# Layer 1 as full masked attention instead of a gather, and layer 3's aggregation as two float32r products instead of one float32 product

## The chip, the cores and the metric

The kernel runs on one core of one Trainium2 chip. The metric is the device time of one execution in microseconds (us). A time given for a kernel is the median of its runs.

## The reference, cut to what matters

There are N = 2708 nodes with D = 512 features, and an adjacency matrix `adj` of 2708x2708 floats in which most entries are zero. Four layers follow each other; each adds to `x` a function of `h = max(layernorm(x), 0)`. All is float32.

```python
# layer 0: inc = adj + head, head the 0/1 mask of adj divided by its row norm
x = x + (inc @ h) / sum(inc, -1)
# layer 1: 8 heads, key size 64; a = max(adj, eye)
atts = einsum('hqk,hmk->hqm', h @ Wq, h @ Wk) / 8
atts = softmax(atts - 1e16 * (1 - a), -1)            # 8 x 2708 x 2708
x = x + einsum('hqm,hmk,hko->qo', atts, h @ Wv, Wo)
# layer 2
g = relu(adj @ (h @ W1) + b1);  g = relu(adj @ (g @ W3) + b3)
x = x + tanh(g @ Wf + bf)
# layer 3: A is 1 where adj is not 0
x = x + (A @ (h @ W + b)) / sum(A, 0)[:, None]
```

In layer 1 the entries of `adj` are weights between 0.05 and 5.42, and the mask term multiplies their differences by 1e16. So in each row the softmax gives weight one to the node with the largest entry, as long as the two largest entries differ by more than the scores can.

## The kernel before, in words

The nodes are cut into 22 tiles of up to P = 128 (21 full ones and one of 20 rows), and into 6 blocks of up to BLK = 512 (five full ones and one of 148). The loops are written out by Python; a list scheduler orders each engine's instructions when the program is built. It prefers the instruction that stands earlier in the program among those whose inputs and buffers are there, and may take later ones while it waits. Each engine then runs its list in order. Pools (`tile_pool`) fix how many buffers a tile has (`bufs`); an instruction waits until a buffer is free. DMAs are issued by SP (`nc.sync`) and POOL (`nc.gpsimd`).

- **Preparation**: `value_weights` (L128) multiplies the value and output weights of layer 1 into one 512x512 matrix `wvo`; `square_sum` (L147) sums the squares of the query and key weights.
- **Layer 0**: first `h0` for all 22 tiles (to L535), then a loop over 22 node tiles `m`. VectorE makes `head` from the slab `at` (L555), counts (`part`, L557), TensorE adds the counts over partitions (`cnt`, L561), VectorE scales and adds (L564 to L574) and sums degrees (`dpart`, L576). TensorE then multiplies the slab with `h0`, 22 products into one accumulator (L583), and `x1` is written (L594).
- **Layer 1 in the same loop**: for tile `m`, the row slab `arow` of `adj` is loaded (L598), its largest entry and index are found (L601, L602), their lead is kept (L603, L611), and the new `x1` is normalised, transposed and multiplied with `wvo` (`accz`, L108), and written to `z` (L622). `alone` (L163) compares the smallest lead with what the scores could differ by, and sets `flag`. Then a loop gathers for each node the row of `z` that its largest entry names (L631), adds `x1` (L642) and writes `x2` (L643).
- **Layers 2 and 3** (`_layers_2_3`): `g1` (tiles of `norm_project`: layernorm, four transposes L102, four products L108); the first aggregation (`aggregate_relu`, L420), block by block, with the projection by `w3`; the second, with the projection by `wf`, tanh, `x3`, and `norm_project` by `w` into `g3`; then the third aggregation (L492) of `g3` with the 0/1 matrix `nz` (L489).
- At the end, `full_attention()` and a second `layers_2_3()` stand inside a conditional block that runs only where `flag` is 0. In the runs shown it isn't entered: no instruction of it is in the trace.

A float32 product is issued as two pairs of LDWEIGHTS and MATMUL; a transpose (a matmul against the identity) as one pair. So `x2112` records at L420 stand for 1056 products.

Of the kernel before, what the change touches and what calls it, by code (L numbers as in the profile page):

```python
# [8 lines left out]
FP = mybir.dt.float32  # L9
AF = mybir.ActivationFunctionType  # L10
# [9 lines left out]
TOP_SLACK = 2.0**-20  # L20
# [3 lines left out]
def kernel(  # L24
# [19 lines left out]

# [67 lines left out]
    z = dram.tile([N, D], FP, name="z")  # L117
    best = const.tile([P, NT, 8], mybir.dt.uint32, name="best")
    lead = const.tile([P, NT], FP, name="lead")
    nc.gpsimd.memset(lead, 1.0)  # L120
    flag = const.tile([1, 1], mybir.dt.int32, name="flag")

    def load_heads(pool, src, name):
        w = pool.tile([P, NCD, D], FP, name=name)
        for h in range(H):
            nc.sync.dma_start(
                out=w[:, :, h * DK : (h + 1) * DK],
                in_=src[h].rearrange("(c p) k -> p c k", p=P),  # L128
            )
        return w  # L130

    def value_weights(wvo, work, psum):

        wv = load_heads(work, wv_d, "wv")
        wo = load_w(work, wo_d, "wo")
        wvT = work.tile([P, NCD, D], FP, name="wvT")
        for c in range(NCD):
            pt = psum.tile([P, NCD, P], FP, name="ptr")
            for j in range(NCD):
                nc.tensor.transpose(pt[:, j, :], wv[:, j, c * P : (c + 1) * P], ident)  # L140
            nc.scalar.copy(wvT[:, c, :], pt.rearrange("p j k -> p (j k)"))
        for j in range(NCD):
            acc = psum.tile([P, D], FP, name="ptr")
            project(acc, wvT[:, :, j * P : (j + 1) * P], P, wo)
            nc.vector.tensor_copy(wvo[:, j, :], acc)

    def square_sum(work):  # L147

        squares = const.tile([P, 2], FP, name="squares")
        for i, (src, name) in enumerate(((wq_d, "wq"), (wk_d, "wk"))):  # L150
            w = load_heads(work, src, name)
            nc.scalar.activation(
                w.rearrange("p c k -> p (c k)"),
                w.rearrange("p c k -> p (c k)"),
                AF.Square,
                accum_out=squares[:, i : i + 1],
            )
        norm = const.tile([P, 1], FP, name="norm")
        nc.vector.tensor_add(norm, squares[:, 0:1], squares[:, 1:2])
        return norm  # L160

    def alone(norm, work, psum):

        total = psum.tile([P, 1], FP, name="ptr")
        nc.tensor.matmul(total, ones, norm, start=True, stop=True)
        least = work.tile([P, 1], FP, name="least")  # L170
        nc.vector.tensor_reduce(least, lead, AX.X, ALU.min)

        spare = work.tile([P, 1], FP, name="spare")
        nc.vector.scalar_tensor_tensor(
            spare,
            total,
            -1.01 * D * float(DK) ** -0.5 / MASK_SCALE,
            least,
            op0=ALU.mult,
            op1=ALU.add,  # L180
        )
        row = psum.tile([P, P], FP, name="ptr")
        nc.tensor.transpose(row[:1, :], spare, ident)
        worst = work.tile([1, 1], FP, name="worst")
        nc.vector.tensor_reduce(worst, row[:1, :], AX.X, ALU.min)
        nc.vector.tensor_scalar(flag, worst, 300.0 / MASK_SCALE, None, op0=ALU.is_gt)

    def full_attention():

        with tc.tile_pool(name="l1_qkv", bufs=1) as qkvp:  # L190
            qT = qkvp.tile([P, NCD, N], FP, name="qT")
            kT = qkvp.tile([P, NCD, N], FP, name="kT")
            v = qkvp.tile([P, NT, D], FP, name="v")
            wo = load_w(qkvp, wo_d, "wo")
            qk_scale = float(DK) ** -0.5

            with tc.tile_pool(name="l1_pw", bufs=1) as pwp, tc.tile_pool(
                name="l1_ph", bufs=2
            ) as php, tc.tile_pool(name="l1_px", bufs=3) as pxp, tc.tile_pool(
                name="l1_pps", bufs=2, space=PSUM  # L200
            ) as ps_tr, tc.tile_pool(name="l1_pacc", bufs=4, space=PSUM) as ps_acc:
                wq, wk, wv = (
                    pwp.tile([P, NCD, D], FP, name=name) for name in ("wq", "wk", "wv")
                )
                for w, src in ((wk, wk_d), (wq, wq_d), (wv, wv_d)):
                    for h in range(H):
                        nc.sync.dma_start(
                            out=w[:, :, h * DK : (h + 1) * DK],
                            in_=src[h].rearrange("(c p) k -> p c k", p=P),
                        )  # L210
                for b in range(NB):
                    c0 = b * BLK
                    nb = min(BLK, N - c0)
                    hT = php.tile([P, NCD, BLK], FP, name="hT")
                    tiles = range(c0 // P, (c0 + nb + P - 1) // P)
                    for t in tiles:
                        n = rows(t)
                        o = t * P - c0
                        xt = pxp.tile([P, D], FP, name="xt")
                        nc.sync.dma_start(out=xt[:n], in_=x1[t][:n])  # L220
                        hn = pxp.tile([P, D], FP, name="hn")
                        layernorm(pxp, xt, n, hn)
                        transpose_relu(ps_tr, hn, n, hT[:, :, o : o + n])
                    for dst, w, scale in ((kT, wk, None), (qT, wq, qk_scale)):
                        for oc in range(NCD):
                            acc = ps_acc.tile([P, BLK], FP, name="acc")
                            for c in range(NCD):
                                nc.tensor.matmul(
                                    acc[:, :nb],
                                    w[:, c, oc * P : (oc + 1) * P],  # L230
                                    hT[:, c, :nb],
                                    start=(c == 0),
                                    stop=(c == NCD - 1),
                                )
                            if scale is None:
                                nc.vector.tensor_copy(dst[:, oc, c0 : c0 + nb], acc[:, :nb])
                            else:
                                nc.scalar.mul(dst[:, oc, c0 : c0 + nb], acc[:, :nb], scale)
                    for t in tiles:
                        n = rows(t)  # L240
                        acc = ps_acc.tile([P, D], FP, name="acc")
                        project(acc, hT[:, :, t * P - c0 : t * P - c0 + n], n, wv)
                        nc.any.tensor_copy(v[:n, t, :], acc[:n])

            with tc.tile_pool(name="l1_bias", bufs=2) as bp, tc.tile_pool(
                name="l1_p", bufs=2
            ) as pp, tc.tile_pool(name="l1_pT", bufs=3) as ptp, tc.tile_pool(
                name="l1_x", bufs=1
            ) as xp, tc.tile_pool(name="l1_st", bufs=4) as stp, tc.tile_pool(
                name="l1_s", bufs=2, space=PSUM  # L250
            ) as ps_s, tc.tile_pool(name="l1_t", bufs=2, space=PSUM) as ps_t, tc.tile_pool(
                name="l1_o", bufs=1, space=PSUM
            ) as ps_o, tc.tile_pool(name="l1_y", bufs=1, space=PSUM) as ps_y:
                SW = 2 * BLK
                for m in range(NT):
                    n = rows(m)
                    cols = slice(m * P, m * P + n)

                    bias = bp.tile([P, N], FP, name="bias")
                    nc.sync.dma_start(out=bias[:n], in_=adj[cols])  # L260
                    xt = xp.tile([P, D], FP, name="xt", bufs=2)
                    nc.sync.dma_start(out=xt[:n], in_=x1[m][:n])
                    nc.vector.tensor_max(bias[:n, cols], bias[:n, cols], ident[:n, :n])
                    nc.vector.tensor_scalar(
                        bias[:n], bias[:n], 1.0, MASK_SCALE, op0=ALU.subtract, op1=ALU.mult
                    )
                    sums = stp.tile([P, H], FP, name="sums")
                    acc_o = ps_o.tile([P, D], FP, name="acc_o")
                    for h in range(H):
# [415 lines left out]
```

## Time and profile before

| | us |
|---|---|
| median of 3 runs | 2511.19 (2510.17 to 2511.49) |
| the profiled execution | 2511.49 |
| its span, first to last instruction | 2509.7 |
| busy in the span: PE / VectorE / ScalarE / POOL | 2185.8 / 896.2 / 172.5 / 76.3 |
| last `z` written by POOL (L622), start of the issue | 847.4 |
| first instruction of TensorE in layer 2 | 914.6 |
| last product of the first two aggregations' stage ends (L429) | 2049.7 |
| last product of layer 3 starts (L492) | 2491.8 |

The mean granted TensorE clock over the span is 0.918. A group of instructions is given by line, engine, operation and the names of what it writes and reads; the two figures behind it are its busy time in us and the mean length of one record in ns. TensorE's records overlap[...]; so the rate of a row of products is read from their starts, not from their lengths.

### The profile page before, as it was taken

The numbers are of one execution on the slowest core, as the hardware profiler recorded it, in microseconds if no ns is written. First come the engines' busy times: TensorE is split into PE (matmuls) and PEld (weight loads), VectorE is DVE, ScalarE is ACT, GpSimd is POOL, SyncE is SP. The second block draws the span as 40 slices with busy tenths as digits, with TensorE's granted clock in tenths as the row PEclk, the third lists the DMA queues.
The fourth block names the chain that finished last, engine by engine and source line by source line (L and its number), as shares of the span: only waits on it lengthen the run. The fifth ranks groups of instructions, "written<-read, shape, count | busy, mean of one in ns | idle before, by whom it ended". The sixth has DMA issues, their size and how long they took to land.

```text
span 2509.7 us, 13959 instructions
## 1 busy us (share of the span) xinstructions
PE 2185.8 (87%) x5331; PEld 968.8 (39%) x5331; DVE 896.2 (36%) x1243; ACT 172.5 (7%) x322; POOL 76.3 (3%) x142
## 2 busy tenths in 40 slices
PE   4776767877778449999999999999999999999997
PEld 2222323333333124444444464444444464444441
DVE  5999995556653153112111110210202021111111
ACT  2100000000000011000000000120202120000000
POOL 0000000000000210000000000000000000000000
PEclk8788878888888769999999999999999999999998
DMA  8545332112220471121222122221222121333311
GB/s 239 169 141 198 127 113 70 51 57 70 70 62 20 163 267 56 51 69 58 64 63 63 46 69 76 88 84 51 71 64 84 47 87 56 105 122 101 105 50 43
DMA packets 161867, 225.24 MB, mean 90 GB/s; under 512 B 23906, under 2 KB 88898, under 8 KB 159084
## 3 DMA queue, kind: packets, MB, share of 16 engines
q1 hardware_dynamic: 153232, 196.53, 25.5%
q0 software_dynamic: 8560, 27.74, 3.0%
q8 instruction: 44, 0.72, 0.1%
q14 instruction: 31, 0.25, 0.0%
HBM read 195.45 MB, written 28.78 MB: 89 GB/s over the span
## 4 chain that ended last, share of the span: by engine, by line
issue 61%; PE 27%; DVE 7%; DMA 3%; POOL 2%; SPq 0%; ACT 0%; POOLq 0%; DVEq 0%; ACTq 0%
PE agg L420 19%; PE pj L108 7%; DVE top L601 1%; DVE part L557 1%; DMA xt<-x 1%; DVE best L602 1%; PE ptr L108 1%; DVE stats L87 1%; DVE dpart L576 1%; DVE at L574 0%; POOL out_dram L505 0%; POOL x L469 0%; POOL x L594 0%; DVE hn L94 0%; PE ptr L102 0%
## 5 line engine op out<-in xcount | busy, mean ns | idle before, releaser
L420 PE MATMUL agg<-a,g 128*128 128x512 f32 (+3 forms) x2112 | 809.8, 543 | 0.0
L583 PE MATMUL acc<-h,at 128*128 128x512 f32 (+1 forms) x968 | 477.7, 645 | 202.1 <-DVE at L574 183.9
L420 PEld LDWEIGHTS agg<-a,g 128*128 128x128 f32 (+1 forms) x2112 | 376.6, 190 | 417.6 <-issue 417.6
L492 PE MATMUL agg<-g,nz 128*128 128x512 f32 x968 | 428.1, 600 | 0.0
L583 PEld LDWEIGHTS acc<-h,at 128*128 128x128 f32 (+1 forms) x968 | 186.5, 200 | 439.8 <-issue 233.8
L492 PEld LDWEIGHTS agg<-g,nz 128*128 128x128 f32 x968 | 176.3, 187 | 250.9 <-issue 244.3
L410 DVE TENSOR_SCALAR_CACHE_REDUCE nz<-a 128x512 f32<-128x512 f32 (+2 forms) x132 | 75.5, 618 | 336.4 <-DMA a<-in_adj_t_dram 336.2
L489 DVE TENSOR_SCALAR nz<-a 128x512 f32<-128x512 f32 (+2 forms) x132 | 52.0, 395 | 368.5 <-PE agg L492 347.3
L465 DVE TENSOR_TENSOR z<-pj,bf 128x512 f32<-128x512 f32 (+1 forms) x22 | 15.2, 691 | 409.2 <-PE pj L108 408.8
L108 PE MATMUL pj<-w,hTt 128*128 128x512 f32 (+1 forms) x352 | 157.4, 600 | 1.1 <-ACT hTt L103 1.0
L102 PE MATMUL ptr<-ident,hn 128*128 128x128 f32 (+1 forms) x264 | 44.3, 311 | 82.0 <-DVE hn L94 82.0
L557 DVE TENSOR_REDUCE part<-head 128x128 f32<-128x2816 f32 (+1 forms) x22 | 105.2, 4781 | 0.4
L576 DVE TENSOR_REDUCE dpart<-at 128x128 f32<-128x2816 f32 (+1 forms) x22 | 104.3, 4741 | 0.0
L108 PEld LDWEIGHTS pj<-w,hTt 128*128 128x128 f32 (+1 forms) x352 | 65.7, 188 | 87.4 <-issue 79.1
L429 ACT ACTIVATE hT<-agg,b 128x512 f32<-128x512 f32 (+1 forms) x48 | 29.8, 637 | 883.8 <-PE agg L420 803.2
L108 PE MATMUL accz<-wvo,hT 128*128 128x512 f32 (+1 forms) x176 | 88.3, 649 | 0.7 <-ACT hT L103 0.7
L108 PE MATMUL pj<-wf,hT 128*128 128x512 f32 (+1 forms) x176 | 88.3, 665 | 0.0
L102 PEld LDWEIGHTS ptr<-ident,hn 128*128 128x128 f32 (+1 forms) x264 | 36.9, 164 | 120.5 <-issue 120.1
L108 PE MATMUL pj<-w,hT 128*128 128x512 f32 (+1 forms) x176 | 82.3, 628 | 0.0
L589 DVE RECIPROCAL rdeg<-deg 128x1 f32<-128x1 f32 (+1 forms) x22 | 3.5, 159 | 209.6 <-PE deg L587 209.6
L574 DVE TENSOR_TENSOR at<-at,head 128x2816 f32<-128x2816 f32 (+1 forms) x22 | 65.5, 2976 | 0.0
L601 DVE MAX8 top<-arow 128x8 f32<-128x2708 f32 (+1 forms) x22 | 65.5, 2976 | 0.0
(77 smaller groups left out, 848.7 us busy)
## 6 DMA issues: line engine op xcount, KB each, us to landing
a<-in_adj_t_dram SPq DMA_DIRECT2D x105, 768.0 KB
arow<-in_adj_dram SPq DMA_DIRECT2D x21, 1354.0 KB
at<-in_adj_t_dram SPq DMA_DIRECT2D x21, 1344.0 KB
xt<-x SPq DMA_DIRECT2D x63, 256.0 KB
xt<-in_x_dram SPq DMA_DIRECT2D x42, 256.0 KB
x<-xo POOLq DMA_DIRECT2D x42, 256.0 KB, 3.8
z<-zo POOLq DMA_DIRECT2D x21, 256.0 KB, 2.3
x<-xo SPq DMA_DIRECT2D x21, 256.0 KB
```

Source lines behind the costliest of these rows:

```text
L102: nc.tensor.transpose(pt[:, c, :n], hn[:n, c * P : (c + 1) * P], ident[:n, :n])
L108: nc.tensor.matmul(acc[:n], hT[:, c, :n], w[:, c, :], start=(c == 0), stop=(c == NCD - 1))
L410: nc.vector.tensor_scalar(nz[:k, :nb], a[:k, :nb], 0.0, None, op0=ALU.not_equal, op1=ALU.add, accum_out=degp[:k, t, block : block + 1],)
L420: nc.tensor.matmul(accs[c][:, :nb], g[:k, t, c * P : (c + 1) * P], a[:k, :nb], start=(t == 0), stop=(t == NT - 1),)
L429: nc.scalar.activation(hT[:, c, :nb], accs[c][:, :nb], AF.Relu, bias=bias[:, c : c + 1])
L489: nc.vector.tensor_scalar(nz[:k, :nb], a[:k, :nb], 0.0, None, op0=ALU.not_equal)
L492: nc.tensor.matmul(accs[m][:n], nz[:k, o : o + n], g3[:k, t, :], start=(t == 0), stop=(t == NT - 1),)
L557: nc.vector.tensor_reduce(part[:, :n], head[:, :, :n].rearrange("p t m -> p m t"), AX.X, ALU.add)
L574: nc.vector.tensor_tensor(at[:, :, :n], at[:, :, :n], head[:, :, :n], ALU.add)
L576: nc.vector.tensor_reduce(dpart[:, :n], at[:, :, :n].rearrange("p t m -> p m t"), AX.X, ALU.add)
L583: nc.tensor.matmul(acc[:n], at[:k, t, :n], h0[:k, t, :], start=(t == 0), stop=(t == NT - 1))
L601: nc.vector.max(top[:n], arow[:n])
```

## The change

Three things change.

1. **Layer 0's loop is left with layer 0 alone.** The preparation, `arow` and its maximum, the layernorm, `accz`, `z`, `flag` and the gather are gone. The pools become deeper: `at` has 3 buffers instead of 2, `head` 2 instead of 1, `cnt` and `deg` 2 instead of 1.
2. **Layer 1 is computed in full, in the main line.** The body of `full_attention` stands where the gather stood, with no condition: for each block `q`, `k` (transposed) and `v` are projected; then for each tile `m` and each of 8 heads the scores of 128 nodes against 2708 are made in 3 pieces (K = 64 rows), VectorE adds the mask and takes the maximum, ScalarE the exponential, TensorE transposes the 22 pieces and multiplies each with its 64 columns of `v`. The conditional block is gone.
3. **Layers 2 and 3** have other pools, and layer 3 splits its features:

```diff
-        gp = es.enter_context(tc.tile_pool(name="g", bufs=2))
-        wp = es.enter_context(tc.tile_pool(name="wp", bufs=3))
-        hp = es.enter_context(tc.tile_pool(name="hp", bufs=2))
-        GRP = 3
+    gp = ctx.enter_context(tc.tile_pool(name="g", bufs=3))
+    wmats = ctx.enter_context(tc.tile_pool(name="wmats", bufs=2))
+    wp = ctx.enter_context(tc.tile_pool(name="wp", bufs=2))
+    hp = ctx.enter_context(tc.tile_pool(name="hp", bufs=1))
+    GRP = 2
...
-                norm_project(xo, rows(t), w, g3[: rows(t), t, :], bl)
+            acc = norm_project(xo, n, w)
+            hid = wp.tile([P, D], FP, name="hid")
+            nc.vector.tensor_add(hid[:n], acc[:n], bl[:n])
+            nc.scalar.copy(hi[:n, t, :], hid[:n])
+            nc.vector.tensor_sub(lo[:n, t, :], hid[:n], hi[:n, t, :])
...
-                nz = wp.tile([P, BLK], FP, name="nz", bufs=2)
+            nz = wp.tile([P, BLK], FR, name="nzr", tag="nz", bufs=2)
...
+            width = len(nodes) * P
+            if width > nb:
+                nc.gpsimd.memset(nz[:k, nb:width].bitcast(FP), 0.0)
             for m in nodes:
-                    n, o = rows(m), m * P - c0
-                    nc.tensor.matmul(
-                        accs[m][:n],
-                        nz[:k, o : o + n],
-                        g3[:k, t, :],
-                        start=(t == 0),
-                        stop=(t == NT - 1),
-                    )
+                o = m * P - c0
+                for half in (hi, lo):
+                    nc.tensor.matmul(
+                        accs[m],
+                        nz[:k, o : o + P],
+                        half[:k, t, :],
+                        start=(t == 0 and half is hi),
+                        stop=(t == NT - 1 and half is lo),
+                    )
         for m in nodes:
-                xo = wp.tile([P, D], FP, name="xo", bufs=4)
+            xo = wp.tile([P, D], FP, name="xf", tag="hid")
```

`hi` and `lo` are float32r (`FR`), both 22 tiles of 128x512. `hi` is the rounding of `hid` to float32r, `lo` what is left of it. The groups of adjacency tiles that one DMA brings shrink from 3 to 2. The loads of `wf` and `w` stand behind the first aggregation, since `wmats` has two buffers for four matrices.

The loop of one head, which now runs 22 x 8 = 176 times:

```python
for s0 in range(0, N, SW):                       # 1024, 1024 and 660 columns
    s = ps_s.tile([P, SW], FP, name="s")         # 2 buffers
    ...  # two products of up to 512 columns, K = 64
    nc.vector.tensor_add(p[:n, s0 : s0 + sw], s[:n, :sw], bias[:n, s0 : s0 + sw])
nc.vector.reduce_max(nmax[:n], p[:n], axis=AX.X)
nc.vector.tensor_scalar_mul(nmax[:n], nmax[:n], -1.0)
nc.scalar.activation(p[:n], p[:n], AF.Exp, bias=nmax[:n], accum_out=sums[:n, h : h + 1])
for t0 in range(0, NT, 4):                       # 6 groups of up to 4 pieces
    ...  # transposes into pt (2 buffers)
    copy = nc.scalar.copy if (t0 // 4) % 2 else nc.vector.tensor_copy
    ...  # copy pt to pT (3 buffers), then one product with v (64 columns) for each piece
```

`p` has 2 buffers, so that of three heads in a row the first must be transposed before the third's scores are stored.

## The prediction

> **What bounds the kernel now.** I read the page's slices first, then its groups, then the chain of waits for the rates of long rows of products, then the timeline of one step of layer 0 and of the gather.
>
> ```profile
> PE   4776767877778449999999999999999999999997
> DVE  5999995556653153112111110210202021111111
> PEclk8788878888888769999999999999999999999998
> ```
>
> Each digit is a 40th of 2509.7 us, 62.7 us. Up to slice 13 (840 us, layer 0) TensorE is neither full nor at full clock; slice 14 is the gather; from slice 15 on TensorE is full. So layers 2 and 3 are bound by TensorE; layer 0 isn't yet explained.
>
> ```profile
> L420 PE MATMUL agg<-a,g 128*128 128x512 f32 (+3 forms) x2112 | 809.8, 543 | 0.0
> L583 PE MATMUL acc<-h,at 128*128 128x512 f32 (+1 forms) x968 | 477.7, 645 | 202.1 <-DVE at L574 183.9
> L492 PE MATMUL agg<-g,nz 128*128 128x512 f32 x968 | 428.1, 600 | 0.0
> L557 DVE TENSOR_REDUCE part<-head 128x128 f32<-128x2816 f32 (+1 forms) x22 | 105.2, 4781 | 0.4
> L465 DVE TENSOR_TENSOR z<-pj,bf 128x512 f32<-128x512 f32 (+1 forms) x22 | 15.2, 691 | 409.2 <-PE pj L108 408.8
> L601 DVE MAX8 top<-arow 128x8 f32<-128x2708 f32 (+1 forms) x22 | 65.5, 2976 | 0.0
> ```
>
> The third figure is the idle time ahead of a group: L420 and L492 wait for nothing, layer 0's L583 waits 183.9 us for VectorE's `at`.
>
> ```profile
> 990.65 0.87 PE ptr L102 x8
> ...
> 1095.77 75.72 PE agg L420 x176
> ```
>
> The chain of waits gives rates: 176 records in 75.72 us, 0.430 us each, so 0.86 us for a float32 product of 512 columns (0.854 from record to record inside a row), and 0.109 us for a transpose.
>
> ```profile
> 532.19 0.38 PE L587 MATMUL deg<-ones,dpart 128*128 128x1 f32 x2
> 532.44 0.47 PE L561 MATMUL cnt<-part,ones 128*128 128x128 f32 x2
> 541.46 2.08 PE L583 MATMUL acc<-h,at 128*128 128x512 f32 x2 [8.56 <-DVE at L574]
> ...
> 566.63 0.47 PE L561 MATMUL cnt<-part,ones 128*128 128x128 f32 x2
> ```
>
> This timeline of TensorE is one step of layer 0: 34.2 us from `cnt` to `cnt`, with 8.56 us in which TensorE waits for VectorE's scaling (L564 to L574). VectorE had the next `part` ready at 553, but `cnt` stands behind the 22 products of this tile. The two one-column records of L587 take 0.38 us at 0.26 each: two weight loads of 128 columns follow each other in about 0.11 us.
>
> ```profile
> 847.36 0.51 POOL L622 DMA_DIRECT2D z<-zo  x1 [10.16 <-ACT zo L621]
> ...
> 914.64 1.09 PE L102 MATMUL ptr<-ident,hn 128*128 128x128 f32 x4 [68.22 <-DVE hn L94]
> ```
>
> The gather costs 914.6 - 842 = 72 us with TensorE idle.
>
> [...] around each 8.56 us wait the granted clock is 0.5 for 10.2 us. [...]
>
> **The change, part by part.** The profiled execution is 2511.5, 1.8 over its span and 0.3 over the median. Before: layer 0 842, gather 72, layers 2 and 3 1595; sum 2509.
>
> *Layer 0.* The preparation goes (the first 31 us, partly under loads). Start: 22 layernorms of 1.5 us on VectorE (33), 4 for the first load, and tile 0's own chain of 14 (1.6, 4.9, 1.3, 3.1, 3.1): its products start at 51, end at 71. After that VectorE needs 19 us a tile (cmp 1.6, part 5.0, rn 1.2, scale 3.1, add 3.1, dpart 4.9, rest), TensorE 18.8 (44 x 0.427) and 0.5. With `head` doubled, VectorE can bring `part` two tiles ahead, so `cnt` of two tiles goes in one pause. While a tile's products are all ready they still go ahead of a later `cnt`, so I count one pause of 8.5 for two tiles, and a cold start of 1.7: 18.8 + 0.5 + (8.5 + 1.7)/2 = 24.4. Layer 0: 71 + 21 x 24.4 = 583. Bounds: never a pause 480; one for every tile 690. `accz`, `z`, `arow`'s DMAs and TensorE's 3.85 us a tile are gone from it.
>
> *Projections q, k, v.* Five blocks of 48 products of 0.854 us (41 each), the last block 32 of 0.247 and 8 of 0.854: 220 us, TensorE bound; copies are under it. Start (a load, a layernorm, weights in pieces of 256 bytes) and clock dips 15: **235**.
>
> *Attention.* On SP it adds a row slab of 1.39 MB a tile, some 109 us apart, with nothing behind it but the next one; `x2` goes from SP (L643) to POOL, one a tile: both hidden, and 5 us a tile if a slab came late. For each head and tile, TensorE: scores 5 x 0.854 + 0.247 (148 columns) = 4.52; 22 transposes x 0.109 = 2.40; 22 products of 64 columns, two records each, where the loads of 128 columns (0.107) outlast the 64 columns: 4.71. A tile adds 4 transposes and 4 products with `wo`, 3.85, or 0.48 a head: 12.1. VectorE: adds from PSUM of 1024, 1024, 660 columns 1.22 + 1.22 + 0.85[...]; the maximum over 2708 columns 2.98 (L601); 0.16; three copies of 0.69; 8.5, with the tile's mask and output 8.9. ScalarE: exponential [...]2.54, its accumulator 0.19, copies 1.7: 4.4. TensorE is the busiest.
>
> It doesn't run without pauses: the chain from the last score to the first transpose is 0.85 + 2.98 + 0.16 + 2.73 + handoffs of 0.8, 7.5 us; the next head's scores fill it (4.5 us, two pieces in PSUM), as later tiles' work filled pauses in layer 0. A copy that VectorE owes may stand behind a running maximum of 2.98. Going through two heads by hand in this order, TensorE loses about 1.3 a head; clock dips 0.2: 13.6. 168 heads x 13.6 = 2285; the tile of 20 rows, with short weights, 88; first head's chain 12: **2385**. Bounds: 12.3 a head (2165) and 16.5 (2890).
>
> *Layers 2 and 3.* Layer 3: 22 x 22 products of 0.854 become 968 float32r ones. Their price from both sides: [...]0.214, sum 207, a gain of 206; or the 0.427 of a float32 record, gain 0. [...]loads of 0.107 are under it. Smaller groups of `a`: 256 KB in 1.7 us, 150 GB/s, where slices reached 267; hidden. `xf` has 2 buffers, and the third node's waits for the output's landing (4.1 us): the accumulator of the next block is late by 4 us at 5 borders, 20. One buffer of `hTt`: relu waits for the product before, hidden by aggregation (0.86 us pieces between the projections); 40 if that cover fails. `wf`, `w` loaded later, behind `a` on SP: needed 75 us after, 5 each if not hidden. `hi`, `lo`: 1.3 us a tile under the aggregation, exposed once. Memset on POOL in one block, 5. Start: 8 after the last head. 1595 - 206 + 33 = **1422**.
>
> Sum: 583 + 235 + 2385 + 1422 + 1.8 = 4627, say 4625.
>
> **The rivals.** *Heads run one after another*, if the order puts no next scores into the chain: 4.5 + 7.5 + 8 + cold clock 2 = 22 a head, 168 x 8.4 = 1411 more: 6035. For it: chain of 7.5, in-order engines. Against: the built order of before goes to later tiles while it waits. *float32r at 0.427*: 206 more, 4830; nothing in this trace speaks for or against it[...]. *Half clock in attention*[...]: TensorE's 12.1 doubles, 25 a head with the pauses, 168 x 11.4 = 1915 more: 6540; against it, the clock is 1.0 in the stretch of transposes and projections at 990. *Not slower*: the attention isn't executed, or hides entirely. After the rest (2242) it has 269 us, 1.53 us a head; from there it decides. VectorE alone has 8.9, and even the exponential 2.54, so only a program that goes around the attention would do: 583 + 1422 + 1.8 = 2007.
>
> **How the numbers follow.** Likeliest case 0.72 (its own range 4290 to 5250), float32r slow 0.11, serial 0.12, half clock 0.04, not slower 0.01. The range 4280 to 5300 holds the first, but for 0.02, and the second: 0.81. It takes in layer 0 from 500 to 690 and a head from 12.3 to 16.5. About 0.2% is what can be told from no change. Slower by more 0.99, faster 0.005, the same 0.005.
>
> **What would show it.** Right: layer 0 in steps of pairs, one long and one short pause of L583, and its end near 580; TensorE about 9 in the attention's slices at full clock with 13 to 14 us from exponential to exponential; transposes 0.11 apart; `agg<-hi` records 0.21 apart and layer 3 near 230 us. Wrong: the exponential's spacing near VectorE's 9 or over 17, clock 0.5 in the attention, or `lo` products at 0.43.

## The result and the profile after

| | us |
|---|---|
| median after | 4678.5 (4671.7 to 4689.8, 4 runs) |
| median before, on the same chip | 2511.1 (4 runs) |
| after / before | 1.864, 95% interval 1.859 to 1.868 |
| the profiled execution after | 4672.5, its span 4670.7 |

In the experiments below, an execution that is over 1.5% longer than the fastest of its version counts in the median and the range given, but not in the ratio.

The page's slices after, each 116.8 us long:

```profile
PE   4888799999999999999999999998999999999998
DVE  8867721366666666666666666664311111111222
PEclk9888899799999999999999999996999999999999
```

The ninth to the 27th digit lie wholly in the attention. TensorE is as full there as in layers 2 and 3, at full clock, and VectorE is at 6 tenths. Its groups on the page are L306, L273 and L295; L172 is layer 0 and L495 layer 3 (busy us, mean ns, idle ahead):

```profile
L306 PE MATMUL acc_o<-v,pT 128*128 128x64 f32 (+2 forms) x7744 | 1001.2, 280 | 100.9 <-DVE pT L301 90.4
...
L273 PE MATMUL s<-kT,qT 64*128 64x512 f32 (+3 forms) x2112 | 789.6, 580 | 5.7 <-DVE p L280 5.0
...
L172 PE MATMUL acc<-h,at 128*128 128x512 f32 (+1 forms) x968 | 452.3, 627 | 121.8 <-DVE at L163 105.7
L295 PE MATMUL pt<-ident,p 128*128 128x128 f32 (+2 forms) x3872 | 531.7, 277 | 1.2 <-ACT p L286 1.2
...
L495 PE MATMUL agg<-hi,nzr 128*128 128x512 f32 x484 | 198.4, 410 | 13.1 <-DVE xf L505 12.7
```

In 176 heads TensorE waits 90 us for VectorE's copies of the transposed `p` (L301) and next to nothing for the scores or the exponential. Layer 0's wait for `at` is 106 us, where it was 184.

Cut by stage (start and end of a stretch, then its us; busy us and records of TensorE's products, its loads, VectorE, ScalarE and POOL; granted clock; DMA share; GB/s), in the order layer 0, projections, attention, the first two aggregations, layer 3, and two stretches inside the attention:

```profile
0.00:624.20 624.20, 465.05 (x1056) 197.55 (x1056) 441.99 (x307) 27.03 (x73) 16.58 (x51) 0.89 0.29 81
624.20:862.70 238.50, 235.29 (x648) 112.01 (x648) 38.59 (x91) 42.09 (x84) 0.52 (x1) 0.99 0.08 24
862.70:3250.00 2387.30, 2279.01 (x13990) 1637.39 (x13991) 1487.23 (x1517) 750.60 (x1080) 11.54 (x22) 0.97 0.05 18
3250.00:4403.00 1153.00, 1136.37 (x2971) 527.08 (x2969) 225.85 (x564) 119.17 (x195) 11.86 (x22) 0.98 0.24 70
4403.00:4670.70 267.70, 244.73 (x993) 188.71 (x992) 73.75 (x165) 4.58 (x8) 16.53 (x45) 0.94 0.48 143
869.90:931.30 61.40, 59.95 (x182) 39.83 (x182) 28.69 (x28) 12.38 (x15) 0.00 (x0) 0.50 0.01 3
3191.00:3249.00 58.00, 53.57 (x298) 30.75 (x297) 21.39 (x29) 10.89 (x23) 0.21 (x1) 0.50 0.13 37
```

| stage | predicted | measured |
|---|---|---|
| layer 0 | 583 | 624.2 |
| projections | 235 | 238.5 |
| attention | 2385 | 2387.3 |
| layers 2 and 3 | 1422 | 1420.7 |

One head of the attention on TensorE, from the timeline:

```profile
1605.60 2.84 PE L273 MATMUL s<-kT,qT 64*128 64x512 f32 x6
1608.37 2.00 PE L306 MATMUL acc_o<-v,pT 128*128 128x64 f32 x16
1610.20 0.83 PE L295 MATMUL pt<-ident,p 128*128 128x128 f32 x6
1611.66 1.69 PE L306 MATMUL acc_o<-v,pT 128*128 128x64 f32 x12 [0.63 <-DVE pT L301]
1613.28 1.09 PE L295 MATMUL pt<-ident,p 128*128 128x128 f32 x8
1614.30 1.38 PE L273 MATMUL s<-kT,qT 64*128 64x512 f32 x6
1615.61 2.00 PE L306 MATMUL acc_o<-v,pT 128*128 128x64 f32 x16
1617.44 1.04 PE L295 MATMUL pt<-ident,p 128*128 128x128 f32 x8
1618.42 2.84 PE L273 MATMUL s<-kT,qT 64*128 64x512 f32 x6
```

The list puts scores of a later head (L273) between the transposes (L295) and the products with `v` (L306) of this one; from one row of 2.84 to the next is a head, 12.82 us. The only wait shown is 0.63 for a copy. The two rows of scores have six records each, but the second takes 1.31 us to the next start and the first 2.77. The second holds the last 660 columns of one head (records of 512 and 148) and the first 512 of the next, and the kernel lays neighbouring heads into different halves of the 128 rows. In the trace the records of its two products of 512 columns start 0.014 us apart, twice: they run at once.

### The profile page after: what moved, and what is told of

Read it like the earlier page. It is cut to its first block, busy times and chain, and to the rows that moved or that the text cites. A ratio compares the mean times of both kernels' runs of the same rounds, so it can differ in the third digit from the quotient of the medians.

```text
span 4670.7 us, 46241 instructions
## 1 busy us (share of the span) xinstructions
PE 4360.5 (93%) x19656; PEld 2662.7 (57%) x19656; DVE 2267.4 (49%) x2644; ACT 943.5 (20%) x1439; POOL 57.0 (1%) x141
## 4 chain that ended last, share of the span: by engine, by line
issue 60%; PE 34%; DVE 4%; DMA 1%; POOL 1%; ACT 0%; SPq 0%; POOLq 0%; DVEq 0%; ACTq 0%
PE agg L408 12%; PE acc L172 9%; PE pj L102 4%; PE acc L224 3%; PE acc L102 2%; DVE head L157 1%; PE agg L495 1%; PE acc_o L306 1%; PE s L273 1%; DVE at L163 1%; PE pt L295 1%; DMA xt<-x 0%; DVE part L146 0%; DVE rn L154 0%; DVE stats L81 0%
## 5 line engine op out<-in xcount | busy, mean ns | idle before, releaser
L306 PEld LDWEIGHTS acc_o<-v,pT 128*128 128x128 f32 (+2 forms) x7744 | 917.5, 190 | 333.6 <-DVE pT L301 149.3
L306 PE MATMUL acc_o<-v,pT 128*128 128x64 f32 (+2 forms) x7744 | 1001.2, 280 | 100.9 <-DVE pT L301 90.4
L273 PE MATMUL s<-kT,qT 64*128 64x512 f32 (+3 forms) x2112 | 789.6, 580 | 5.7 <-DVE p L280 5.0
L280 DVE TENSOR_TENSOR p<-s,bias 128x1024 f32<-128x1024 f32 (+1 forms) x528 | 565.1, 1090 | 198.9 <-PE s L273 183.2
L301 DVE COPY pT<-pt 128x512 f32<-128x512 f32 (+1 forms) x528 | 352.1, 667 | 558.9 <-PE pt L295 539.2
L172 PE MATMUL acc<-h,at 128*128 128x512 f32 (+1 forms) x968 | 452.3, 627 | 121.8 <-DVE at L163 105.7
L295 PE MATMUL pt<-ident,p 128*128 128x128 f32 (+2 forms) x3872 | 531.7, 277 | 1.2 <-ACT p L286 1.2
L284 DVE TENSOR_REDUCE nmax<-p 128x1 f32<-128x2708 f32 (+1 forms) x176 | 523.2, 2973 | 5.3
L301 ACT COPY pT<-pt 128x512 f32<-128x512 f32 (+1 forms) x528 | 246.1, 466 | 1351.7 <-PE pt L295 1350.4
L286 ACT ACTIVATE p<-p,nmax 128x2708 f32<-128x2708 f32 (+1 forms) x176 | 449.2, 2552 | 237.5 <-DVE nmax L285 237.4
L273 PEld LDWEIGHTS s<-kT,qT 64*128 64x128 f32 (+1 forms) x2112 | 301.6, 185 | 324.7 <-issue 303.8
L295 PEld LDWEIGHTS pt<-ident,p 128*128 128x128 f32 (+2 forms) x3872 | 428.4, 147 | 40.3 <-issue 25.8
L172 PEld LDWEIGHTS acc<-h,at 128*128 128x128 f32 (+1 forms) x968 | 186.1, 197 | 372.3 <-issue 251.5
L495 PE MATMUL agg<-hi,nzr 128*128 128x512 f32 x484 | 198.4, 410 | 13.1 <-DVE xf L505 12.7
L495 PE MATMUL agg<-lo,nzr 128*128 128x512 f32 x484 | 194.7, 402 | 0.0
```

Of the source, the lines that this page charges most:

```text
L172: nc.tensor.matmul(acc[:n], at[:k, t, :n], h0[:k, t, :], start=(t == 0), stop=(t == NT - 1))
L273: nc.tensor.matmul(s[:n, j0 : j0 + jw], qT[r0 : r0 + DK, oc, cols], kT[r0 : r0 + DK, oc, s0 + j0 : s0 + j0 + jw], start=True, stop=True,)
L280: nc.vector.tensor_add(p[:n, s0 : s0 + sw], s[:n, :sw], bias[:n, s0 : s0 + sw])
L284: nc.vector.reduce_max(nmax[:n], p[:n], axis=AX.X)
L286: nc.scalar.activation(p[:n], p[:n], AF.Exp, bias=nmax[:n], accum_out=sums[:n, h : h + 1])
L295: nc.tensor.transpose(pt[:k, t - t0, :n], p[:n, t * P : t * P + k], ident[:n, :n])
```

## The experiments

**1. The split of layer 3 alone.** The kernel before, with layers 2 and 3 as after; the gather and the conditional second pass stay.

> The kernel before with one part of the change alone: the last two layers as the changed kernel has them (float32r halves, its pools), layer 1 still a gather. If the split gains what its own stage shows, layer 3 from the last product of the second aggregation to the end takes 268 us instead of 453: 185 less, 2326 us. If the shallower pools of layers 2 and 3 cost something that the attention hid, it is 2345 or more; if float32r gained nothing, 2511 or a little above.

Measured: 2322.4, ratio 0.924 (0.923 to 0.926): 188 us less than the 2510.5 of the kernel before on the same chip. So the split of layer 3, with the pools that come with it, is a gain, and the loss lies elsewhere.

**2. The changed kernel without the split.**

```diff
-        hi = gp.tile([P, NT, D], FR, name="hi", tag="g")
-        lo = gp.tile([P, NT, D], FR, name="lo", tag="g")
+        g3 = gp.tile([P, NT, D], FP, name="g")
...
-                for half in (hi, lo):
-                    nc.tensor.matmul(accs[m], nz[:k, o : o + P], half[:k, t, :], ...)
+                nc.tensor.matmul(accs[m][:n], nz[:k, o : o + n], g3[:k, t, :], ...)
```

> The changed kernel with the split undone: features in one float32 tensor, one float32 product instead of two float32r ones, all else as it is. By the stage's own times 185 us more, 4863 us; the first theory of the prediction (0.214 us for a float32r record) would make it 206 more, 4885; if the pauses between blocks eat the gain, less than 100 more.

`nz` is float32 again, and the rounding and the difference are gone.

Measured: 4853.1, ratio 1.931 (1.924 to 1.937): the split is worth 175 here, against 188 in experiment 1. Both are near the 206 that a float32r record of 0.214 us would gain (in the changed kernel it takes 0.230), and exclude the rival of 0.427, which gains nothing.

**3. The changed kernel without layer 1.** `x2 = x1`; the projections and the attention are left out.

> The changed kernel without layer 1: projections and attention left out, layer 2 reads the output of layer 0. If layer 1 stands alone in time, as the stages show (624 us before it, 1421 behind it), 2055 us or up to 15 more for the start of layer 2. If layers 0 and 2 had been stretched by it or partly hidden under it, 2100 or more, or under 2030.

Measured: 2025.8, ratio 0.807 (0.805 to 0.809). Layer 1 costs 4678.5 - 2025.8 = 2653 us: the 238.5 and 2387 of its stages and 27 more, most of it at the start of layer 2. There, in the timelines of the changed kernel (first) and of this one, layer 2 starts so:

```profile
3265.67 1.94 PE L96 MATMUL ptr<-ident,hn 128*128 128x128 f32 x8 [14.43 <-DVE rstd L87]
```

```profile
626.55 1.07 PE L96 MATMUL ptr<-ident,hn 128*128 128x128 f32 x8 [0.34 <-DVE rdeg L178]
```

After the attention, layer 2 waits 14.4 us for its first layernorm; without the attention it waits 0.3. The granted clock is 0.50 from 3256 to 3268, and the first eight records take 1.94 instead of 1.07. So the start that I had as 8 is 14.4 plus a cold start.

**4. One buffer for `p`.** It takes away what lets a next head's scores into this head's chain, so that it makes the rival of serial heads.

```diff
-            name="l1_p", bufs=2
+            name="l1_p", bufs=1
```

> The changed kernel with one buffer for the scores p instead of two, so that a head's scores can be stored only when the head before is transposed. If the second buffer is what lets one head's scores fill the other's chain, a head costs 20 to 22 us instead of 13.3, and the kernel 5800 to 6150 us. If TensorE's work alone sets the pace, the order mattering little, it stays below 4850.

Measured: 6611 (two runs), ratio 2.633 (2.628 to 2.639); 25 us a head. Its TensorE, from the timeline and in a stretch:

```profile
2013.33 7.28 PE L273 MATMUL s<-kT,qT 64*128 64x512 f32 x12
2022.77 1.97 PE L295 MATMUL pt<-ident,p 128*128 128x128 f32 x8 [2.16 <-ACT p L286]
2024.73 3.67 PE L306 MATMUL acc_o<-v,pT 128*128 128x64 f32 x16
```

```profile
1100.00:2700.00 1600.00, 1398.90 (x5142) 999.38 (x5141) 561.45 (x556) 279.13 (x396) 4.33 (x8) 0.56 0.03 10
```

Scores take 7.28 us, and 16 records with `v` 3.67 instead of 2.00: the clock is 0.56. The second buffer is what hides the chain; without it the serial order costs more than the 22 us that I gave the rival, because TensorE is also at half clock.

**5. Less work for VectorE in a head.**

```diff
-MASK_SCALE = 1e16
+MASK_SCALE = 1.0
...
-                    nc.vector.reduce_max(nmax[:n], p[:n], axis=AX.X)
+                    nc.vector.reduce_max(nmax[:n], p[:n, :256], axis=AX.X)
```

With most of the maximum left out and the old scale, arguments of the order of 1e16 could reach the exponential; scaling the mask takes 1.56 us with the old factor and 1.57 with the new one.

> Layer 1's maximum is taken over the first 256 columns of the scores only and the mask is scaled by 1, so this kernel leaves out most of the maximum and computes other numbers; VectorE has some 2.5 us less to do in each of the 176 heads, TensorE the same. Theory (TensorE's records fill the head): a head goes from 13.3 to at least 12.5 us, the time falls by 0 to 140 us, to 4540-4680. Rival (the chain through the maximum fills the head): each head loses the 2.5 us, 176 x 2.5 = 440 us, to about 4240.

Measured: 4686 (4664 to 4762), ratio 1.860 (1.854 to 1.866), where the changed kernel has 1.864 (1.859 to 1.868): nothing gained that stands clear of the noise. The profiled execution is the longest of the five, with a longer half-clock stretch at the attention's start (215 us instead of 61).

**6. Less work for TensorE in a head.**

```diff
-                        for t in ts:
+                        for t in ts if t0 not in (4, 8, 12) else ():
                             k = rows(t)
                             nc.tensor.matmul(acc_o[:n, h * DK : (h + 1) * DK], ...)
```

> Layer 1 leaves out the products of p with v for 12 of the 22 tiles of columns (24 of the 44 records of 0.112 us a head); the transposes, the copies and everything on VectorE and ScalarE stay. Theory (TensorE's records fill the head): a head loses 24 x 0.112 = 2.7 us, 176 heads lose 473 us, about 4205 (4050 to 4400, since the planner lays TensorE's order out anew). Rival (the chain of scores, maximum, exponential and copies fills the head, TensorE's records lie beside it): above 4600.

Measured: 4553, ratio 1.817 (1.810 to 1.825): 125 less, not 473, and not nothing. Neither expectation held; a head may have two limits close together.

**7. Both cuts at once** tests that.

> Both cuts at once in layer 1: the maximum over the first 256 columns only with the mask scaled by 1 (2.5 us a head less on VectorE, most of the maximum left out), and the products of p with v left out for 12 of 22 tiles (2.7 us a head less on TensorE). Theory (two limits stand close together in a head, TensorE's records and the chain through VectorE's maximum, so that each cut alone left the other in force): a head falls from 13.3 to about 10.6 us, about 4205 (4150 to 4330). Rival (the order in which the planner lays out TensorE's work, or its clock, takes back what is cut): above 4450.

Measured: 4254, ratio 1.693 (1.689 to 1.696), 425 less, where the cuts alone gave nothing and 125. So each cut left something in force that the other takes away. The same stretch of the attention, in the changed kernel, then 5, 6 and 7 (columns as in the table of stages):

```profile
1100.00:2700.00 1600.00, 1530.18 (x9498) 1114.78 (x9498) 1016.51 (x1030) 512.55 (x730) 8.09 (x15) 1.00 0.05 18
```

```profile
1100.00:2700.00 1600.00, 1600.00 (x9352) 1088.06 (x9351) 719.66 (x1011) 499.55 (x719) 7.55 (x14) 1.00 0.05 18
```

```profile
1100.00:2700.00 1600.00, 1533.14 (x7094) 948.97 (x7093) 1087.00 (x1103) 545.61 (x783) 8.67 (x16) 0.89 0.06 20
```

```profile
1100.00:2700.00 1600.00, 1600.00 (x8067) 963.83 (x8066) 882.07 (x1254) 615.92 (x889) 9.71 (x18) 1.00 0.06 21
```

With the short maximum TensorE is busy for 1600.00 of 1600 us, in 5 and in 7. Between those two only TensorE's records differ, and a tile of 8 heads goes from 109.0 to 88.1 us (from one write of `x2` to the next): 2.6 us a head for 24 records of 0.112, 2.7. With the full maximum the same cut (6) leaves tiles of 92 to 108 us, 99.9 in the mean. TensorE idles 0.52 us a head, waiting for the maximum and the copies, and the clock is at half for 437 of the 1998 us of 20 tiles. Counted by transposes, a head takes 11.75 us at full clock and 15.9 at half, against 11.0 in 7. So the second limit has two parts of about the same size: what VectorE does to TensorE's waits and order, and the clock. Why the clock falls in 6 is not shown: the changed kernel idles as much (69.8 of the 1600 us above, 66.9 in 6) and is at full clock in this stretch.

The cuts have a side effect. The scheduler orders TensorE's list by its own costs, so each edit in a head gives another list. In the changed kernel a head's scores take 4.17 us (from the start of a record to the next start, over four tiles in the middle of the attention); in 5 they take 5.06. There they go mostly in pairs between other records, 0.52 instead of 0.43 apart, and the products of two heads that run at once are fewer: a score record starts within 0.06 us of another 133 times in 176 heads, against 319 times in the changed kernel. What its transposes no longer wait (2.78 us a head instead of 3.40) is spent there, so 5 is not a little faster than the changed kernel. I have not run the short maximum in the old order; the 0.58 us a head that TensorE idles in the changed kernel would be some 100 us in all (an estimate).

**8. Products with `v` of 128 columns.** The count of products and loads is the same; half of each product's columns belong to the neighbouring head.

```diff
-                                acc_o[:n, h * DK : (h + 1) * DK],
+                                acc_o[:n, oc * P : (oc + 1) * P],
...
-                                v[:k, t, h * DK : (h + 1) * DK],
+                                v[:k, t, oc * P : (oc + 1) * P],
```

> The products of p with v are made 128 columns wide instead of 64 (other columns of v come in with them, so the numbers differ); the count of products and of weight loads stays. Theory (a product of 64 columns takes the 0.11 us of its weight load, not of its columns): within 1%, 4640-4730. Rival (the time goes by the columns): 44 products a head x 0.05 us x 176 heads = 390 us more, about 5070.

Measured: 4769, ratio 1.898 (1.895 to 1.901), 90 more, between the two. The median distance of these records is 0.112 us as before, so twice the columns cost nothing inside a row, and the price by columns falls. But the list is another: over four tiles a head takes 14.06 us instead of 13.33, its scores 5.07 instead of 4.17 (129 of all its score records start within 0.06 us of another), the products 5.45 instead of 5.26, and the transposes 3.04 instead of 3.40. So most of what is added lies in the scores, which the edit does not touch; I have not run the wide products in the old order.

**9. All copies of `p` on ScalarE.**

```diff
-                        copy = nc.scalar.copy if (t0 // 4) % 2 else nc.vector.tensor_copy
+                        copy = nc.scalar.copy
```

> All copies of the transposed p out of PSUM are on ScalarE instead of in turn on ScalarE and VectorE. Theory (the remaining 0.5-1 us a head is TensorE waiting for copies that stand behind VectorE's maxima): heads fall from 12.8 to about 12.3 us, 50 to 90 us less, 4590-4630. Rival (copies then stand behind ScalarE's exponential of 2.55 us and ScalarE takes on 3 us a head): the same or slower, 4680-5100.

Measured: 4877, ratio 1.943 (1.937 to 1.949), 199 more: the rival's side in time, but not by its mechanism. A tile takes 110.4 us instead of 106.7, some 80 for all; half-clock stretches of 215 us at the start and 113 in the middle, where after has 61, take (215 + 113 - 61)/2 = 134 (an estimate). TensorE's waits for copies have all but gone, as the theory had it (13.7 us between 1000 and 3000, where the changed kernel has 80.0). The 80 lie in the order instead: a head's scores take 5.18 us instead of 4.17, and only 21 score records in all start within 0.06 us of another.

**10. Layer 0 with the pools of before.**

```diff
-        name="l0_slab", bufs=2
+        name="l0_slab", bufs=1
...
-    ) as ps_acc, tc.tile_pool(name="l0_small", bufs=2, space=PSUM) as ps_small:
+    ) as ps_acc, tc.tile_pool(name="l0_small", bufs=1, space=PSUM) as ps_small:
...
-            at = slabs.tile([P, NT, P], FP, name="at", bufs=3)
+            at = slabs.tile([P, NT, P], FP, name="at", bufs=2)
```

> Layer 0's pools have the buffer counts of the kernel before (slab 1, at 2, small 1), the rest is the changed kernel. Theory (layer 0's time is products of 19.3 us a tile and one pause for each two tiles, which the buffers let go in pairs; with fewer buffers there is a pause for each tile): 22 tiles at about 30 us instead of 26.4, +60 to +100 us, 4740-4780. Rival (the buffers are not what sets layer 0): 4660-4700.

Measured: 4741, ratio 1.885 (1.881 to 1.889), 62 more. Its step, from the timeline:

```profile
311.52 0.47 PE L150 MATMUL cnt<-part,ones 128*128 128x128 f32 x2
320.08 21.99 PE L172 MATMUL acc<-h,at 128*128 128x512 f32 x44 [8.09 <-DVE at L163]
342.00 0.38 PE L176 MATMUL deg<-ones,dpart 128*128 128x1 f32 x2
342.25 0.47 PE L150 MATMUL cnt<-part,ones 128*128 128x128 f32 x2
```

30.7 us for each tile with one pause and one cold row in each. The deeper pools are what lets `cnt` go in pairs.

**11. A version that beats both.** Experiment 1 with a third buffer for `xf`, and layer 0's `head` with 2 and `at` with 3 buffers.

> The kernel before with layer 3's float32r split, and in addition a third buffer for layer 2/3's normalised tiles and layer 0's head and at pools with one buffer more each; the gather of layer 1 stays. Theory (layer 0's pauses come from its mask chain and buffers; the pauses at block borders from the output's DMA): 30 to 90 us below the 2322 of the split alone, 2230-2290. Rival (VectorE sets the pauses, more buffers change nothing): 2310-2335.

Measured: 2231.1, ratio 0.888 (0.886 to 0.890). What TensorE waits for in experiment 1, and then here:

```profile
PE acc L595 <- DVE at L586: 187.7, 21, 14.8
...
PE agg L504 <- DVE xf L514: 13.0, 5, 3.5
```

```profile
PE acc L595 <- DVE at L586: 43.6, 6, 10.2
...
PE agg L504 <- DVE xf L514: 5.4, 4, 1.6
```

144 us of layer 0's waits and 8 of layer 3's are gone, though other waits take some of it back (those of the transposes for `rstd` and `hn` go from 63 to 131 us): the time fell by 91.

## Why the prediction was right, and where it was off

Of the 54 us between 4625 and 4678.5, 41 are layer 0, and 6 lie between the profiled execution and the median.

**Attention, 2385 against 2387.** The steps held: transposes 0.109 from record to record, products with `v` 0.112 (I had 0.107), heads 12.8 us apart with a tile's output on top. The adds of 1024 and of 660 columns take 1.214 and 0.846 in the mean, the exponential 2.552 and its accumulator 0.186; the 1.22, 0.85, 2.54 and 0.19 that I had for them were estimates that the lines of before quoted in the prediction do not show. The total agrees by luck, because errors cancel. The 20 tiles after the first take 2141 us, 107.1 each, where 8 x 13.6 gave 108.8: 35 less. The first tile, to its write, takes 152 instead of 121: the 61.4 us at half clock would cost half of themselves, 31 (an estimate). The tail tile is 94 instead of 88, at half clock for its 58 us.

Inside a head, luck helped too. The prediction had 12.1 us of records and 1.3 of waits for VectorE. Over four tiles a head takes 13.33: TensorE idles 0.58 of it, and its records take 12.76, 0.50 of them the tile's output. Products with `v` take 5.26 where the sum had 4.71, transposes 2.83 without the idle time where it had 2.40. Scores take 4.17 where it had 4.52, because the sum had them one after another, and in most heads two products run at once. So the waits were priced at twice what they were, and the records too low.

The reason given, "TensorE is the busiest", was right in what it said and less safe than it sounded. VectorE's 8.9 us a head (8.5 in the trace, 271.54 in 32 heads) looks like a third in hand, but its maximum must end before the exponential, and its copies stand behind the maximum. Experiments 6 and 7 show what that leaves: with fewer products a head takes 11.75 us at full clock with the full maximum, 11.0 with the short one.

**Serial heads.** The mechanism was real (experiment 4) and under-priced: 25 us, not 22. The half clock that I had as a rival of its own came with it.

**Layer 0, 583 against 624: the term that was mis-sized is the pause.** It goes in pairs, as forecast. A pair, first TensorE and then VectorE from the timeline after:

```profile
232.79 19.32 PE L172 MATMUL acc<-h,at 128*128 128x512 f32 x44
252.29 0.69 PE L150 MATMUL cnt<-part,ones 128*128 128x128 f32 x4
264.36 21.80 PE L172 MATMUL acc<-h,at 128*128 128x512 f32 x44 [11.38 <-DVE at L163]
```

```profile
255.28 6.02 DVE L157 TENSOR_TENSOR head<-head,rn 128x2816 f32<-128x2816 f32 x2
261.22 6.09 DVE L163 TENSOR_TENSOR at<-at,head 128x2816 f32<-128x2816 f32 x2
```

In the pause of a pair VectorE scales both tiles before it adds the first, so one more scaling of 3.0 stands ahead of the products: 11.4, not 8.5. The cold row (granted clock 0.50 from 256 to 268) costs 21.8 - 19.3 = 2.5, not 1.7, and a row takes 19.3, not 18.8. A pair takes 53.5 us from `cnt` to `cnt` (252.29 to 305.83), 26.8 a tile. The first and the last pause are shorter (6.3 and 8.4), so in the mean a step is (624.2 - 81)/21 = 25.9 instead of 24.4, 31 us; the products of the first tile end at 81 instead of 71, 10 us.

**Layers 2 and 3, 1422 against 1421.** A float32r record takes 0.230 us instead of 0.214: 968 x 0.016 is 15 more. The 0.214, a quarter of the 0.854 of a float32 product, was an assumption of mine: no float32r product runs in the kernel before. From its first product to its last, layer 3 takes 258 us, where the prediction said near 230 and counted the pauses at the borders apart. At the borders of blocks, TensorE and then VectorE:

```profile
4456.53 0.50 PE L495 MATMUL agg<-hi,nzr 128*128 128x512 f32 x1 [2.20 <-DVE xf L505]
...
4458.61 0.80 PE L495 MATMUL agg<-hi,nzr 128*128 128x512 f32 x1 [0.80 <-DVE xf L505]
```

```profile
4455.73 0.75 DVE L505 SCALAR_TENSOR_TENSOR xf<-agg,rdeg,x3t 128x512 f32<-128x512 f32 x1 [2.96 <-DMA out_dram<-xf]
```

The wait for the output's landing is there, 3 us here where I had 4, and behind it the granted clock is 0.50 from 4458 to 4464, with records 0.43 apart instead of 0.23. TensorE waits 12.7 us in all for `xf`, where I had 20. With the start (14.4, not 8) this is within a few us of what I had, and nothing of the 40 for `hTt` showed: TensorE waits 2.1 us for it.

## What to carry to other kernels

Price a new stage by its busiest engine, then ask which chain stands next: cut each in a throw-away version, alone and together. If the two together pay far more than each alone, the stage has two limits; then look whether the second is a wait or the clock. And where a scheduler writes the order, an edit that changes one cost changes the order of all engines: compare the lists before the difference is put down to the edit.

## What the runs showed of the hardware that was not expected

- The clock stayed at half for 61.4 us from 869.9 on, in the attention's start. There was one wait of 4.8 us at its beginning; in the stretch TensorE is busy 59.95 of 61.40. In experiments 5 and 9 the same start stayed at half for 215 us, in 8 it lasted under 25. The prediction counted on a return within a few us of work, as in layer 0 before (10.2 us at half clock around a wait of 8.56, some 3.6 of them after TensorE had started again at 541.46); that does not hold here. What ends the stretch I can't say.
- In experiment 6 the clock falls to half for 27 us at a time, again with TensorE nearly full (26.64 of 27.00 between 2652 and 2679), and the clock takes more than the waits there: 0.74 us a head (12.49 in the mean, 11.75 at full clock), against 0.52 of idle time. Why it falls is open.
- A score record of 512 columns and 64 rows takes 0.43 us in a longer row and 0.52 in a lone pair between other records.
- Score products of two neighbouring heads, which use different halves of the 128 rows, ran at once where the list put them side by side: in the row at 1614.30 their records start 0.014 us apart, and six records (four of 512 columns, two of 148) take 1.31 us, where the row at 1605.60 takes 2.77 for six of 512. The kernel does no more for it than to slice `qT` and `kT` by head.
